# A gated cross-attention and feed-forward block: the down product's way out of PSUM, and its inputs' gather

## The chip, the cores and the metric

The kernel runs on one core of a Trainium2 chip. The metric is the device time of one execution in microseconds (us), lower is better. A core has a tensor engine (PE, with its weight loads PEld), a vector engine (DVE), a scalar engine (ACT), a general engine (POOL) and a sync engine (SP), each with its own queue of instructions, and DMA queues.

## What is computed

The inputs are `x` and a context, each of 8 batches of 256 rows by 512 channels, four 512 x 512 attention weights with biases, and three feed-forward weights of width 1408 with two index lists. Cut to what matters:

```
x = x + tanh(g_xattn) * cross_attention(layernorm(x), context)     # 16 heads, int8-like projections
x = x + tanh(g_ffn)   * ffn(layernorm(x))

ffn(x), rows flattened to 2048 x 512:
    qx, sx, sc = quantise(x, up_index)         # channels reordered, fp8 grid, one scale for each row
    g = (qx*sx) @ (gate weights)^T * sc        # both reordered and quantised, a scale for each column
    u = (qx*sx) @ (up weights)^T * sc
    t = silu(g) * u                            # 2048 x 1408
    qt, st, sct = quantise(t, down_index)      # fp8 grid, st: one scale for each row
    y = (qt*st) @ (qw*w_scale)^T * sct         # w_scale: one scale for each column of y
```

So the last product is multiplied by a number for each row, `st`, and by a number for each column, `w_scale`, and then added to the residual `x`.

## The kernel before

The kernel has two stages. In the first, a loop over batches and pairs of heads computes the attention, and between its steps it prepares the feed-forward weights and, for each batch, the quantised input of the feed-forward part (`quantise_x2`, L743). That input is transposed (channels on partitions), and `store` (L767) writes it to a scratch tensor in device memory, `scr_x[b]`, of 512 channels by 256 rows in bf16.

The second stage is the loop from L1029 over tiles of 128 rows, t = 0 to 15, two tiles to a batch, with two more turns to drain. Three tiles are in work at once. In turn t the kernel does the gate and up products of tile t, the quantisation of tile t-1 and the down product of tile t-2. The order in each engine's queue is the order of the list `steps`: the handles `pe`, `dve`, `act`, `pool` (class `InOrder`) keep the program's order. Instructions outside of these handles, those of the attention's end (`behind_heads`, one step after each turn), are placed between them by the framework. The steps:

- `gather_x` (L912): channels in the order of the index list are fetched from `scr_x[b]` into the tile `xg` by an indirect DMA from POOL's queue; four for a batch, each of 128 channels by 256 rows. Two are issued in each turn, for a tile three turns later; six stand ahead of the loop. `xg` has three buffers.
- `product` (L927): PE, 704 of the 1408 columns at a time, into one of two PSUM buffers of two banks.
- `scaled` (L942): DVE takes a product out of PSUM with the row's scale and the columns' scales (`s_gate`, `s_up`).
- `silu` (L955) on ACT, `sl`; then `gated` (L960) on POOL multiplies it with `s_up` into `tt`.
- `largest` (L971), DVE: `mxt`, the largest magnitude of each row of `tt`; `st`, the scale; `rs_t`, its reciprocal; and `sy`, `st` times the constant UNIT.
- `grid_parts` (L983), ACT: `v_t` and `a_t`. `grid_whole` (L990), DVE: `q_t` and `qt`, the quantised rows.
- `turned` (L997): PE transposes `qt` into PSUM (`ptq`), ACT copies it out as `qtT` in two pieces.
- `down` (L1007): PE, 11 matmuls into one PSUM bank, `yp`.
- `finished` (L1015): DVE takes `yp` out of PSUM, times `sy` of the row, times `scales["down"]` of the column, into `yo`; POOL adds the residual; SP's queue sends 128 rows to the output.

Some order within turn t, as far as the change touches it: first halves of `scaled`, `silu`, `gated`; `gather_x`; `largest` and `grid_parts` of t-1; `down` of t-2; second halves; `grid_whole` and `turned` of t-1; last `finished` of t-2.

`down_scales` (L852) prepares the column scales in the first stage, times the tanh of the gate.

Of the kernel before, what the change touches and what calls it, by code (L numbers as in the profile page):

```python
# [29 lines left out]
F32 = mybir.dt.float32  # L30
BF16 = mybir.dt.bfloat16
# [3 lines left out]
AF = mybir.ActivationFunctionType  # L35
ALU = mybir.AluOpType
# [4 lines left out]
P = 128  # L41
# [4 lines left out]
R448 = 1.0 / 448.0  # L46
F8_MAX = 240.0
UNIT = 1.0 / (F8_MAX / 2) ** 2
# [18 lines left out]
def tile_flamingo_block(  # L67
# [22 lines left out]
    nc = tc.nc  # L90
    B, S, C = x.shape
# [4 lines left out]
    KC = C // P  # L96
    IC = I // P
    TPB = S // P
# [12 lines left out]
    dram = ctx.enter_context(tc.tile_pool(name="dram", bufs=1, space=DRAM))  # L111

    def ctile(shape, name, dt=F32):
        return const.tile(shape, dt, tag=name, name=name)
# [9 lines left out]
    gate = ctile([P, 2], "gate")  # L124
# [26 lines left out]
    for k in range(IC):  # L151
        nc.gpsimd.indirect_dma_start(
            out=dd_i[:, k : k + 1],
            out_offset=None,
            in_=down_idx.rearrange("(r e) -> r e", e=1),
# [14 lines left out]
    }  # L170
    scr_d = dram.tile([I, C], BF16, tag="scr_d", name="scr_d")
    held_d = [dram.tile([I, 1], BF16, tag=f"held{k}", name=f"held{k}") for k in range(IC)]
    scr_x = [dram.tile([C, S], BF16, tag=f"scr_x{b}", name=f"scr_x{b}") for b in range(B)]

    def fp8_grid(rp, src, rs, dst, n, name, v_bufs=3):

        v = rp.tile([P, n], F32, tag="r_v", name=f"v_{name}", bufs=v_bufs)
        nc.scalar.activation(v, src, AF.Identity, scale=rs)
        a = rp.tile([P, n], FP8, tag="r_a", name=f"a_{name}")
        nc.scalar.activation(a, v, AF.Abs, scale=0.5, saturate=False)  # L180
        q = rp.tile([P, n], FP8, tag="r_q", name=f"q_{name}")
        nc.vector.tensor_scalar(q, v, F8_MAX, -F8_MAX, ALU.min, ALU.max, saturate=False)
        nc.vector.scalar_tensor_tensor(dst, a, F8_MAX / 2, q, ALU.max, ALU.mult)

    def scale_of(pool, mx, s, name):

        nc.vector.tensor_scalar(s, mx, R448, None, ALU.mult)
        rs = pool.tile([P, s.shape[-1]], F32, tag="rs", name=f"rs_{name}")
        nc.vector.reciprocal(rs, s)
        return rs  # L190
# [8 lines left out]
    def absmax(dst, src):  # L199
        nc.vector.tensor_reduce(dst, src, AX.X, ALU.max, apply_absolute_value=True)  # L200
# [7 lines left out]
    scales = {}  # L208

    def two_banks(name):  # L210
        return ps_h.tile([P, 2, 512], F32, tag="h", name=name)
# [5 lines left out]
    with ExitStack() as actx:  # L217
# [525 lines left out]
        def quantise_x2(b):  # L743

            xT = tl.tile([P, KC, S], BF16, tag="x2T", name=f"x2T_{b}", bufs=1)

            def rows(nt):
                t = b * TPB + nt
                st = sm.tile([P, 6], F32, tag="st", name=f"st2_{t}")
                nc.vector.bn_stats(st, x_sb[:, t, :])  # L750
                mv = sm.tile([P, 2], F32, tag="mv", name=f"mv2_{t}")
                nc.vector.bn_aggr(mv, st)
                nc.vector.tensor_copy(var2[:, t : t + 1], mv[:, 1:2])
                xm = tl.tile([P, C], F32, tag="xm", name=f"xm_{t}", bufs=1)
                nc.vector.scalar_tensor_tensor(  # L755
                    xm, x_sb[:, t, :], mv[:, 0:1], mu_b, ALU.subtract, ALU.mult
                )
                mx = sm.tile([P, 1], F32, tag="mx", name=f"mx2_{t}")
                absmax(mx, xm)
                rs = scale_of(sm, mx, mx2[:, t : t + 1], f"x2_{t}")  # L760
                q2 = tl.tile([P, C], BF16, tag="q8", name=f"q2_{t}", bufs=4)
                fp8_grid(rp, xm, rs, q2, C, f"x2_{t}")
                return partial(
                    transpose_bf16, q2, xT[:, :, nt * P : (nt + 1) * P], KC, f"x2_{t}"
                )

            def store():  # L767
                nc.sync.dma_start(scr_x[b].rearrange("(k p) n -> p k n", p=P), xT)

            return behind([partial(rows, nt) for nt in range(TPB)]) + [store]  # L770

# [80 lines left out]
        def down_scales():  # L852
            scales["down"] = sd_b = wp.tile([P, C], F32, tag="wqT", name="sd_b")
            row_bcast(sd_b, s_d, "sd")
            nc.vector.tensor_scalar(sd_b, sd_b, gate[:, 1:2], None, ALU.mult)

# [1 line left out]
        for g in range(B * NP + 2):  # L860
            b, i = divmod(g, NP)
# [34 lines left out]


    with ExitStack() as fctx:
        fx = fctx.enter_context(tc.tile_pool(name="fx", bufs=3))
        fw = fctx.enter_context(tc.tile_pool(name="fw", bufs=2))  # L900
        fs = fctx.enter_context(tc.tile_pool(name="fs", bufs=4))
        pe, dve, act, pool = (
            InOrder(tc, e) for e in (nc.tensor, nc.vector, nc.scalar, nc.gpsimd)
        )
        HI = I // 2
        QI = HI // 2
        xg, tiles = {}, [{} for _ in range(NT)]
# [1 line left out]
        def two(a):  # L909
            return a.rearrange("p (j q) -> p j q", q=QI)  # L910

        def gather_x(t):  # L912

            b, nt = divmod(t, TPB)
            if b >= B:
                return
            if nt == 0:
                xg[b] = fx.tile([P, KC, S], BF16, tag="xg", name=f"xg_{b}")
            for k in range(nt * KC // TPB, (nt + 1) * KC // TPB):
                pool.indirect_dma_start(  # L920
                    out=xg[b][:, k, :],
                    out_offset=None,
                    in_=scr_x[b][:, :],
                    in_offset=bass.IndirectOffsetOnAxis(ap=u_i[:, k : k + 1].bitcast(U32), axis=0),
                )

        def product(t, n, half):  # L927
            b, nt = divmod(t, TPB)
            ph = two_banks(f"p_{n}_{t}_{half}")
            for j in range(2):  # L930
                c0 = half * HI + j * QI
                for k in range(KC):
                    pe.matmul(
                        ph[:, j, :QI],
                        xg[b][:, k, nt * P : (nt + 1) * P],
                        wT[n][:, k, c0 : c0 + QI],
                        start=(k == 0),
                        stop=(k == KC - 1),
                    )
            tiles[t][n, half] = ph  # L940
# [30 lines left out]
        def largest(t):  # L971

            h = tiles[t]
            mx = fs.tile([P, 1], F32, tag="mx", name=f"mxt_{t}")
            dve.tensor_reduce(mx, h["tt"], AX.X, ALU.max, apply_absolute_value=True)
            st = fs.tile([P, 1], F32, tag="st", name=f"st_{t}")
            dve.tensor_scalar(st, mx, R448, None, ALU.mult)
            h["rs"] = fs.tile([P, 1], F32, tag="rs", name=f"rs_t_{t}")
            dve.reciprocal(h["rs"], st)
            h["sy"] = fs.tile([P, 1], F32, tag="sy", name=f"sy_{t}")  # L980
            dve.tensor_scalar(h["sy"], st, UNIT, None, ALU.mult)

        def grid_parts(t):  # L983
            h = tiles[t]
# [30 lines left out]
        def finished(t):  # L1015
            h = tiles[t]
            yo = fw.tile([P, C], F32, tag="yo", name=f"yo_{t}")
            dve.scalar_tensor_tensor(
                yo, h["py"], h["sy"], scales["down"], ALU.mult, ALU.mult
            )  # L1020
            pool.tensor_tensor(yo, yo, x_sb[:, t, :], ALU.add)
            nc.sync.dma_start(of[t * P : (t + 1) * P, :], yo)
            tiles[t] = None

        for t in range(TPB + 1):
            gather_x(t)
        product(0, "gate", 0)
        product(0, "up", 0)
        for t in range(NT + 2):  # L1029
            a, b, c = t < NT, 0 <= t - 1 < NT, 0 <= t - 2 < NT  # L1030
            d = a and t + 1 < NT
            steps = [
                (a, scaled, t, "gate", 0),
                (a, product, t, "gate", 1),
                (a, silu, t, 0),
                (a, scaled, t, "up", 0),
                (a, product, t, "up", 1),
                (a, gated, t, 0),
                (a, gather_x, t + TPB + 1),
                (b, largest, t - 1),  # L1040
                (b, grid_parts, t - 1),
                (c, down, t - 2),
                (a, scaled, t, "gate", 1),
                (d, product, t + 1, "gate", 0),
                (a, silu, t, 1),
                (a, scaled, t, "up", 1),
                (d, product, t + 1, "up", 0),
                (a, gated, t, 1),
                (b, grid_whole, t - 1),
                (b, turned, t - 1),  # L1050
                (c, finished, t - 2),
            ]
            for due, f, *args in steps:
                if due:
                    f(*args)
            if t < len(behind_heads):
                behind_heads[t]()
# [51 lines left out]
```

## Time and profile before

| | us |
|---|---|
| median of 3 runs (lowest, highest) | 666.72 (664.53, 668.69) |
| the profiled execution | 663.05 |
| its span on the core | 661.3 |
| windows 573.5 to 627.0 (tiles in undisturbed turns) | 53.50; DVE busy 50.55, PE 48.57, POOL 42.36, ACT 33.64 |
| first instruction of a tile's product in the loop | 476.5 |
| last DMA issued | 652.6 |

In the span from 476 to 653 us, POOL's groups are: `tt` 32 times, 64.8 us busy in all (mean 2025 ns); the gathers, 26 of the 32, 29.0 us (mean 1116); the residual sums `yo` 16 times, 20.2 us (mean 1266). DVE's `yo` are 16 of 743 ns, `sy` 16 of 133 ns.

How to read the profile: its page gives the busy time of each engine, its share of the span and the number of instructions. A line of the timeline is an instruction or a run of like ones: start, duration (both us from the span's start), engine, line, operation, what is written and read (`out<-in`) with partitions x elements and types, and in brackets how long the engine was idle before it and what released it. Instructions issued by a helper carry the helper's line: all steps of the second stage show L61. Durations of neighbours on DVE and ACT overlap a little, so that costs are better read from start to start.

### The profile page before, as it was taken

To read this page: it belongs to the slowest core of one execution; us is meant where nothing else is said; L and a number is where in the kernel's file an instruction comes from. 1 tells how busy PE (TensorE), PEld (TensorE's weight loads), DVE (VectorE), ACT (ScalarE), POOL (GpSimd) and SP (SyncE) were. 2 spreads that over 40 slices of the span, in tenths; PEclk is the share of its full clock that TensorE was granted. 3 is DMA by queue.
4 is the path that set the end of the run, shared out by engine and by line. 5 is a ranking of instruction groups with operands and counts; after the bars stand their busy time and mean duration, and the time that the engine had idled before them with its cause. 6 is when DMAs were issued, how large, how long until landed. Compare 5 with 4: busy or idle time off the path is not lost.

```text
span 661.3 us, 10435 instructions
## 1 busy us (share of the span) xinstructions
PE 519.1 (79%) x3591; PEld 336.7 (51%) x3591; DVE 523.9 (79%) x1405; ACT 428.4 (65%) x995; POOL 273.4 (41%) x236
## 2 busy tenths in 40 slices
PE   2697787978986996996899695896568786899962
PEld 1565555645843753663575464484345453555530
DVE  1996887598658689789749799889589997999970
ACT  1468978729847966984884797575646556556650
POOL 3454263343342331343122001441366875788541
PEclk9798997995995997798699797999698997999986
DMA  8941022002241200301141210320100010111000
GB/s 220 365 87 34 2 79 65 17 16 67 70 152 48 66 16 17 97 17 32 40 168 63 74 55 35 112 81 2 40 17 25 32 48 24 57 49 33 33 32 32
DMA packets 28268, 41.65 MB, mean 63 GB/s; under 512 B 7884, under 2 KB 15436, under 8 KB 28215
## 3 DMA queue, kind: packets, MB, share of 16 engines
q1 hardware_dynamic: 19974, 28.25, 12.9%
q0 software_dynamic: 4656, 12.20, 6.6%
q10 hardware_dynamic: 3584, 0.54, 0.6%
q8 instruction: 28, 0.46, 0.3%
q14 instruction: 26, 0.20, 0.1%
HBM read 30.33 MB, written 10.65 MB: 62 GB/s over the span
## 4 chain that ended last, share of the span: by engine, by line
DVE 34%; PE 30%; ACT 17%; issue 9%; DMA 4%; POOL 3%; SPq 1%; POOLq 0%; ACTq 0%; DVEq 0%
ACT pr L623 6%; PE pk L486 5%; PE t L639 5%; DVE sn L613 3%; DVE mxt L61 3%; PE pv L502 3%; PE s L598 2%; PE poT L657 2%; ACT pT L648 2%; PE p_gate L61 2%; DVE s_gate L61 2%; PE p_up L61 2%; DVE s_up L61 2%; DVE xm L755 2%; ACT v_t L61 2%
## 5 line engine op out<-in xcount | busy, mean ns | idle before, releaser
L623 ACT ACTIVATE pr<-sn,nm 128x256 f32<-128x256 f32 x256 | 127.6, 504 | 44.9 <-DVE nm L613 44.5
L613 DVE CUSTOM_DVE_ANT_0 sn<-s,mk 128x256 f32<-128x256 f32 x256 | 97.9, 417 | 16.2 <-ACT pr L623 10.0
L639 PE MATMUL t<-ident,pr 128*128 128x128 f32 x512 | 79.6, 299 | 19.9 <-DVE v L509 11.8
L598 PE MATMUL s<-kT,qT 32*128 32x256 f32 x512 | 62.3, 484 | 32.3 <-DVE nm L613 22.7
L61 POOL TENSOR_TENSOR tt<-s_up,sl 128x704 f32<-128x704 f32 x32 | 64.8, 2025 | 45.0 <-ACT sl L61 35.2
L639 PEld LDWEIGHTS t<-ident,pr 128*128 128x128 f32 x512 | 62.5, 153 | 34.9 <-DVE v L509 13.4
L61 PEld LDWEIGHTS <-xg 128*128 128x128 bf16 x512 | 50.8, 100 | 53.2 <-issue 13.0
L648 ACT COPY pT<-t 128x512 f32<-128x512 f32 x120 | 65.2, 585 | 13.7 <-PE t L639 13.6
L486 PE MATMUL pk<-cT,wkT 128*128 128x256 f32 x256 | 66.8, 414 | 6.4 <-ACT cT L479 3.5
L61 PE MATMUL p_gate<-gateT,xg 128*128 128x352 bf16 x256 | 45.7, 324 | 21.4 <-DVE s_gate L61 21.4
L486 PEld LDWEIGHTS pk<-cT,wkT 128*128 128x128 f32 x256 | 50.9, 206 | 20.8 <-ACT kT L493 4.1
L738 POOL TENSOR_TENSOR x_sb<-x_sb,bo_b 128x512 f32<-128x512 f32 x16 | 22.8, 1435 | 90.1 <-ACT xq L527 90.1
L598 PEld LDWEIGHTS s<-kT,qT 32*128 32x128 f32 x512 | 34.9, 220 | 48.1 <-issue 31.2
L502 PE MATMUL pv<-wvT,cT 128*128 128x512 f32 x128 | 58.3, 600 | 0.0
L562 POOL TENSOR_SCALAR qT<-qT,bq_c 128x256 f32<-128x256 f32 x32 | 17.9, 565 | 87.4 <-DVE qT L559 65.7
L623 ACT ACTIVATION_READ_ACCUMULATOR pr<-sn,nm 128x1 f32 x256 | 49.6, 194 | 0.0
L61 PE MATMUL yp<-wdT,qtT 128*128 128x512 bf16 x176 | 44.5, 406 | 1.7 <-ACT qtT L61 1.7
L61 PE MATMUL p_up<-upT,xg 128*128 128x352 bf16 x256 | 44.8, 319 | 0.0
L61 ACT COPY qtT<-ptq 128x1024 bf16<-128x1024 bf16 (+1 forms) x32 | 22.3, 749 | 32.3 <-PE ptq L61 32.3
L61 ACT ACTIVATE v_t<-tt,rs_t 128x1408 f32<-128x1408 f32 x16 | 23.5, 1470 | 28.0 <-DVE sy L61 26.2
L61 POOL DMA_INDIRECT xg<-scr_x,u_i x32 | 35.3, 1104 | 11.1 <-issue 5.8
L657 PE MATMUL poT<-pT,v 128*32 128x256 f32 x512 | 38.4, 423 | 0.5 <-ACT pT L648 0.5
(192 smaller groups left out, 1115.5 us busy)
## 6 DMA issues: line engine op xcount, KB each, us to landing
cr<-in_ctx_dram SPq DMA_DIRECT2D x8, 512.0 KB
x_sb<-in_x_dram SPq DMA_DIRECT2D x8, 512.0 KB
out_dram<-yo SPq DMA_DIRECT2D x16, 256.0 KB
wd<-in_L_ffn_w_down_dram SPq DMA_DIRECT2D x4, 704.0 KB
mk<-in_mask_BxSxS_ff_dram SPq DMA_DIRECT2D x8, 256.0 KB
scr_x<-x2T SPq DMA_DIRECT2D x8, 256.0 KB
scr_gate<-gateT SPq DMA_DIRECT2D x1, 1408.0 KB
scr_up<-upT SPq DMA_DIRECT2D x1, 1408.0 KB
```

What stands on the lines that cost most here:

```text
L61: return self.tc.keep_in_program_order(method(*args, **kwargs))
L486: nc.tensor.matmul(pk[:, :L], wTf["k"][:, cc, oc * P : (oc + 1) * P], cT[:, cc, :], start=(cc == 0), stop=(cc == KC - 1),)
L502: nc.tensor.matmul(pv, cT[:, cc, lt * P : (lt + 1) * P], wTf["v"][:, cc, :], start=(cc == 0), stop=(cc == KC - 1),)
L562: nc.gpsimd.tensor_scalar(qT[:, oc, :], qT[:, oc, :], bq_c[:, oc : oc + 1], ISD, ALU.add, ALU.mult)
L598: return nc.tensor.matmul(pss[h][:, nt, :], qT[r0 : r0 + D, oc, nt * P : (nt + 1) * P], kT[r0 : r0 + D, oc, :], start=True, stop=True,)
L613: nc.vector.tensor_tensor_reduce(out=sn[:, nt, :], in0=pss[h][:, nt, :], in1=mk[:, nt, :], scale=-1.0, scalar=3.0e38, op0=ALU.add, op1=ALU ...
L623: nc.scalar.activation(pr[:, nt, :], sn[:, nt, :], AF.Exp, bias=nm[:, nt : nt + 1], scale=-1.0, accum_out=sums[:, nt, h : h + 1],)
L639: nc.tensor.transpose(pst[:, lc, nt * P : (nt + 1) * P], pr[:, nt, lc * P : (lc + 1) * P], ident,)
L648: nc.scalar.copy(pT, pst)
L657: return nc.tensor.matmul(poT[oc][r0 : r0 + D, :], v[0][:, lc, h * D : (h + 1) * D], probsT[h][:, lc, :], start=(lc == 0), stop=(lc == LC ...
L738: nc.gpsimd.tensor_tensor(x_sb[:, t, :], x_sb[:, t, :], bo_b, ALU.add)
L755: nc.vector.scalar_tensor_tensor(xm, x_sb[:, t, :], mv[:, 0:1], mu_b, ALU.subtract, ALU.mult)
```

## The change

The down product leaves PSUM on ACT instead of DVE: an Identity activation with the row's scale `st`. POOL then multiplies by the columns' scales, in place, and adds the residual as before. The constant UNIT goes from the row's scale (`sy` is gone) into the columns' scales, as the second operation of the instruction that applies the gate. The scratch tensors hold two batches side by side (512 channels x 2 x 256 rows), so that one indirect DMA fetches 128 channels of two batches: `xg` has two buffers of twice the size. Of these gathers four stand ahead of the loop, and two each in the turns 1, 2, 5, 6, 9 and 10.

```diff
-    scr_x = [dram.tile([C, S], BF16, tag=f"scr_x{b}", name=f"scr_x{b}") for b in range(B)]
+    scr_x = [
+        dram.tile([C, 2, S], BF16, tag=f"scr_x{b}", name=f"scr_x{b}") for b in range(B // 2)
+    ]
...
-                nc.sync.dma_start(scr_x[b].rearrange("(k p) n -> p k n", p=P), xT)
+                nc.sync.dma_start(
+                    scr_x[b // 2][:, b % 2, :].rearrange("(k p) n -> p k n", p=P), xT
+                )
...
-            nc.vector.tensor_scalar(sd_b, sd_b, gate[:, 1:2], None, ALU.mult)
+            nc.vector.tensor_scalar(sd_b, sd_b, gate[:, 1:2], UNIT, ALU.mult, ALU.mult)
...
-        fx = fctx.enter_context(tc.tile_pool(name="fx", bufs=3))
+        fx = fctx.enter_context(tc.tile_pool(name="fx", bufs=2))
...
-        def gather_x(t):
-
-            b, nt = divmod(t, TPB)
-            if b >= B:
-                return
-            if nt == 0:
-                xg[b] = fx.tile([P, KC, S], BF16, tag="xg", name=f"xg_{b}")
-            for k in range(nt * KC // TPB, (nt + 1) * KC // TPB):
+        def gather_x(j, k0, k1):
+
+            if k0 == 0:
+                xg[j] = fx.tile([P, KC, 2, S], BF16, tag="xg", name=f"xg_{j}")
+            for k in range(k0, k1):
                 pool.indirect_dma_start(
-                    out=xg[b][:, k, :],
+                    out=xg[j][:, k, :, :].rearrange("p b n -> p (b n)"),
                     out_offset=None,
-                    in_=scr_x[b][:, :],
+                    in_=scr_x[j].rearrange("c b n -> c (b n)"),
                     in_offset=bass.IndirectOffsetOnAxis(ap=u_i[:, k : k + 1].bitcast(U32), axis=0),
                 )
...
-                        xg[b][:, k, nt * P : (nt + 1) * P],
+                        xg[b // 2][:, k, b % 2, nt * P : (nt + 1) * P],
...
-            st = fs.tile([P, 1], F32, tag="st", name=f"st_{t}")
-            dve.tensor_scalar(st, mx, R448, None, ALU.mult)
+            h["st"] = fs.tile([P, 1], F32, tag="st", name=f"st_{t}")
+            dve.tensor_scalar(h["st"], mx, R448, None, ALU.mult)
             h["rs"] = fs.tile([P, 1], F32, tag="rs", name=f"rs_t_{t}")
-            dve.reciprocal(h["rs"], st)
-            h["sy"] = fs.tile([P, 1], F32, tag="sy", name=f"sy_{t}")
-            dve.tensor_scalar(h["sy"], st, UNIT, None, ALU.mult)
+            dve.reciprocal(h["rs"], h["st"])
...
             yo = fw.tile([P, C], F32, tag="yo", name=f"yo_{t}")
-            dve.scalar_tensor_tensor(
-                yo, h["py"], h["sy"], scales["down"], ALU.mult, ALU.mult
-            )
+            act.activation(yo, h["py"], AF.Identity, scale=h["st"])
+            pool.tensor_tensor(yo, yo, scales["down"], ALU.mult)
             pool.tensor_tensor(yo, yo, x_sb[:, t, :], ALU.add)
...
-        for t in range(TPB + 1):
-            gather_x(t)
+        gather_x(0, 0, KC)
...
-                (a, gather_x, t + TPB + 1),
+                (0 < t % 4 < 3 and t // 4 + 1 < B // 2, gather_x, t // 4 + 1, t % 4 * 2 - 2, t % 4 * 2),
```

## The prediction

> **What bounds the kernel now.** I read the page first, then the windows of the last stage, then the timeline of one tile. The page says that the two busiest engines are level and that POOL has room on average:
>
> ```profile
> PE 519.1 (79%) x3591; PEld 336.7 (51%) x3591; DVE 523.9 (79%) x1405; ACT 428.4 (65%) x995; POOL 273.4 (41%) x236
> ```
>
> That mean mixes two stages, and the change touches only the second, the feed-forward loop over 16 tiles (t = 0 to 15, from 476 to 653 us). In the stretch 573.5 to 627 us, six undisturbed tiles, the windows give DVE 50.55 of 53.50 us busy, PE 48.57, POOL 42.36, ACT 33.64. One tile (t = 13) by the timeline; I call the start of its first `s_gate`, 609.13, T:
>
> ```profile
> 609.13 0.94 DVE L61 SCALAR_TENSOR_TENSOR s_gate<-p_gate,s_x,sb_gate 128x704 f32<-128x704 f32 x1
> 609.99 0.94 DVE L61 SCALAR_TENSOR_TENSOR s_up<-p_up,s_x,sb_up 128x704 f32<-128x704 f32 x1
> 610.85 1.61 DVE L61 TENSOR_REDUCE mxt<-tt 128x1 f32<-128x1408 f32 x1
> 612.68 0.16 DVE L61 RECIPROCAL rs_t<-st 128x1 f32<-128x1 f32 x1
> 612.76 0.13 DVE L61 TENSOR_SCALAR sy<-st 128x1 f32<-128x1 f32 x1
> 612.93 1.47 ACT L61 ACTIVATE v_t<-tt,rs_t 128x1408 f32<-128x1408 f32 x1 [1.59 <-DVE sy L61]
> 614.43 1.38 ACT L61 ACTIVATE a_t<-v_t 128x1408 fp8e4<-128x1408 f32 x1
> 614.52 0.88 DVE L61 TENSOR_SCALAR q_t<-v_t 128x1408 fp8e4<-128x1408 f32 x1
> 615.84 1.62 DVE L61 SCALAR_TENSOR_TENSOR qt<-a_t,q_t 128x1408 bf16<-128x1408 fp8e4 x1 [0.44 <-ACT a_t L61]
> 616.57 2.44 POOL L61 TENSOR_TENSOR tt<-s_up,sl 128x704 f32<-128x704 f32 x1 [3.47 <-ACT sl L61]
> 617.38 0.74 DVE L61 SCALAR_TENSOR_TENSOR yo<-yp,sy,sd_b 128x512 f32<-128x512 f32 x1
> 618.05 0.94 DVE L61 SCALAR_TENSOR_TENSOR s_gate<-p_gate,s_x,sb_gate 128x704 f32<-128x704 f32 x1
> 618.18 1.39 ACT L61 COPY qtT<-ptq 128x1024 bf16<-128x1024 bf16 x2 [1.69 <-PE ptq L61]
> 618.97 1.27 POOL L61 TENSOR_TENSOR yo<-yo,x_sb 128x512 f32<-128x512 f32 x1
> ```
>
> The period is 618.05 - 609.13 = 8.92 us and DVE is full except for one gap: `qt` starts 0.03 after ACT's `a_t` ends (615.81), 0.44 after DVE could have. So DVE bounds the tile, with the chain rs, v_t, a_t, qt beside it. POOL's second product `tt` takes 2.44 here against 1.68 where nothing disturbs it: it starts while `qt` runs. That is the second thing to see, since the change gives POOL work. The same conflict with POOL first, and with two POOL operations in a row:
>
> ```profile
> 560.55 3.20 DVE L61 SCALAR_TENSOR_TENSOR qt<-a_t,q_t 128x1408 bf16<-128x1408 fp8e4 x1
> 560.57 1.69 POOL L61 TENSOR_TENSOR tt<-s_up,sl 128x704 f32<-128x704 f32 x1
> ```
> ```profile
> 116.78 2.91 POOL L738 TENSOR_TENSOR x_sb<-x_sb,bo_b 128x512 f32<-128x512 f32 x2 [4.91 <-ACT xq L527]
> 117.08 1.49 DVE L294 TENSOR_SCALAR ri_o<-o,rs_o 128x512 f32<-128x512 f32 x1
> 118.49 1.49 DVE L535 TENSOR_SCALAR qx<-xq 128x512 bf16<-128x512 f32 x1
> ```
>
> `qt` took 3.20 instead of 1.62: it stood still for the whole `tt` (1.69). In the second case DVE's small operations (0.41 alone) took 1.49 each, and both POOL operations together 2.91 instead of 2.54: DVE got in after the first POOL operation although the second was queued, then POOL after that. So the two take turns.
>
> **What the Trainium skill says.** "SBUF — State Buffer", section "Who interferes with whom": DVE operations in a two-port mode, or with two SBUF inputs, and GpSimd operations share one port pair as an exclusive lock for the whole instruction. The trace agrees (3.20 against 1.62). It also says that a DVE operation with one SBUF input is free of it; the trace agrees: `s_gate`, `s_up` (one input in PSUM) and `mxt` keep 0.94 and 1.61 beside POOL. So of DVE's work in a tile only `q_t` and `qt` need the port, and the `yo` that leaves DVE (input in PSUM) never did. "Perfetto Trace Analysis", "Optimizing Scalar/DVE Operations", warns that for this reason offloading from DVE to GpSimd might not help. "ScalarE: Activation LUTs", "Step-by-step: what each stage is for": a per-partition scale goes into the same pass of an ACTIVATE; no run here shows it from PSUM with a scale, see below.
>
> **The change part by part, in one tile.**
> Removed from DVE: `sy`, 0.05 from start to start (612.76 to 612.81), worth nothing, since `qt` waits for `a_t`, whose chain does not hold `sy`; and `yo`, 617.38 to 618.05, 0.67. Alone this gives a period of 8.25.
> Added to ACT: `yo`, 128x512 f32 from PSUM. A COPY of that shape takes 0.585 (L648), of 128x256 0.37 (L669); Identity with a pointer operand at 128x256 0.47 (L493). So 0.585 + 0.10 = 0.68; ends 0.58 and 0.73 (v_x, from SBUF). Its cover: ACT idles 1.6 us before `v_t` and 1.7 before `qtT`. It is queued behind the two `qtT` copies, and behind it wait the next `silu` and with that POOL's `tt`; by the clock below `silu` ends 0.26 before `v_t` is due, and if `yo` took more than that, `v_t`, `a_t` and `qt` would move with it one for one.
> Added to POOL: one 128x512 product, the row of its `yo` sum, 1.27. The second waits for the first on the same engine: I take 0.05 between (DVE shows 0.03 to 0.04). The product waits for ACT, and behind it in POOL's queue stand the sum, the next tile's first `tt`, its gathers and its second `tt`, for which `mxt` waits.
> The clock of the new tile, from T: `ptq` starts 0.14 after T (617.52 less the 617.38 at which `qt` lets the next DVE operation go, which is the new T); `qtT` 0.80; ACT is free 1.28 later, 2.08; `yo` on ACT to 2.76; POOL's product 2.84 to 4.11, sum 4.16 to 5.43, first `tt` after that (its silu ends 3.5). Before, that `tt` ran from 2.29 to 3.97, clear of everything. DVE asks for the port for `q_t` at 5.34. It waits for the sum, runs 5.43 to 6.23; `tt` waits, runs 6.23 to 7.90; `qt`, ready at 6.71, waits until 7.90 and lets go at 9.43. The second `tt` (asked 7.87) runs then, until 1.65 after the new T, just ahead of `mxt` at 1.72. So the period is about 9.42, not 8.25: +0.50 against before. The sum behind it: on the port `q_t` 0.8, `qt` 1.53, two `tt` 3.36, two `yo` 2.54 and the time from 1.65 to 2.84 in which POOL waits for qt, ptq, qtT and yo in turn.
> Seven tiles, t = 9 to 15: 7 x 0.50 = +3.5.
> Tiles 2 to 8 carry the rest of the attention and are longer. `yo` on DVE is on the path in t = 5 and 7 (-0.67 each); in 3 and 4 DVE waits for `py` (L727, behind `ptq`) anyway, in 6 for ACT's table load and Sqrt. Losses: t = 3: POOL's `tt` would run from 511.35 to 513.03, `q_t` wants 511.8, so `qt` lets go 1.2 later; t = 6: ACT's `yo` enters the chain qtT, v_x, table load, +0.7; t = 5: q_x (L182) behind POOL, +0.5; t = 8: +0.3. Together about +1.2, with -1 and +5 as ends, as the port's turns fall.
> End: `yp` ends 650.43, then DVE 0.75, POOL 1.26, DMA at 652.63. New: ACT 0.68, POOL 1.27 twice, 0.05: +1.2. Nothing covers it.
> Gathers: 26 in the loop become 12, twice as long in bytes (128 KB), POOL's time for one taken as before (0.98, and 0.30 between). POOL saves 14 x 1.4 us, in tiles 0, 3, 4, 7, 8, 11, 12. Worth 0: POOL waits 35.2 us for silu in these stages. What it costs: in t = 9 and 10 two gathers still stand before the second `tt`, which then ends 2.5 after T and delays `mxt` by 0.9; `q_t` and `qt` come that much later and miss the first `tt`, so the period stays 9.4. Landing 2.6 us before; up to the 4.2 of `gateT`, first used two tiles later. The last pair waits for batch 7's store, issued at 568.0, gathered after 579; were it late, POOL's `tt` and both `yo` would queue behind it. UNIT in `down_scales`, a longer `st`, and the store's address: 0 (no instruction more; far off the path). Two buffers of 4 KB instead of three of 2: the third pair's buffer is free after tile 3, asked for in 5: 0.
> Sum: 3.5 + 1.2 + 1.2 = +5.9 on the profiled execution's 663.05 (span 661.3 and 1.75 around it): 669.0. That execution lies 3.67 under the median of the runs, so against the median: 666.72 + 5.9 = 672.6.
>
> **Rivals.**
> A, POOL takes two turns. If ACT's `yo` is 0.58, the sum ends at 5.33 and the first `tt` may take the port just before `q_t` asks (5.34). Then `tt` to 7.0, `q_t` to 7.8, the second `tt` (asked at 7.44) to 9.5, `qt` to 11.1: a period of 11.05, 1.6 more, in the tiles with no gather around them (8, 12 to 15): +8.1, 680.7. For it: the tie is 0.1 us wide. Against it: L493's 0.10 for the pointer.
> B, the other side: DVE's relief counts in full. It decides if `q_t` and `qt` find the port free, that is if POOL's product, sum and `tt` end before 5.34 (2.5 us of work from 2.84, not 4.3), or if these operations lock each other less than `qt` at 560.55 did. Then 0.67 in t = 5, 7 and 8 to 15 (10 tiles), 1.6 of the stall at 560.55, in whose tile no gather is left, less 1.2 at the end: -7.1, 659.6. For it: DVE is the bound and ACT and POOL have room on average; against it the rows above.
> C, nothing: long tiles give back what the last seven lose: 667.
>
> **How the numbers follow.** Forecast 0.48 (own range 668.5 to 677.5, by tiles 2 to 8 and ACT's price), A 0.17 (677 to 686), B 0.30 (655 to 664), C 0.05. A measurement of this kernel tells about 1% (6.7 us) from no change. Under 660.0: 0.19 of B. Over 673.4: 0.21 of the forecast and all of A, 0.38. Between: 0.43. The range 658 to 681 leaves out the low end of B (0.10) and the high end of A (0.10).
>
> **What would show it.** Steady period 9.4 from `s_gate` to `s_gate`, with `qt` lasting about 2.7 instead of 1.62 and ending with POOL's first `tt` in front of it; `mxt` not waiting. ACT's `yo` 0.68. A `qt` of 1.62 and a period near 8.25 means B; `qt` after both `tt` and a period near 11 means A. Last DMA 1.2 later after the last `yp`. The forecast is wrong if `q_t` and `qt` run beside POOL undelayed.

## The result, and the profile after

The changed kernel takes 672.40 us in the median of 8 runs (669.70 to 678.34), against 666.32 (663.45 to 668.69) for the kernel before on the same chip: 1.2% slower, ratio 1.0119 with a 95% interval of 1.009 to 1.0148. The profiled execution took 670.81 us, with a span of 669.0; that is 7.7 more than the span before. The medians differ by 6.1.

The page's line of busy times. DVE lost 31 instructions, yet it is busy for as long as before (524.7 against 523.9), ACT and POOL for 9 and 11.5 us more:

```profile
PE 523.3 (78%) x3591; PEld 339.3 (51%) x3591; DVE 524.7 (78%) x1374; ACT 437.4 (65%) x1010; POOL 284.9 (43%) x236
```

The same tile as in the prediction, t = 13, in the timeline of the changed kernel. T, the start of its first `s_gate`, is 615.55; here and below, rows that the reading does not need are left out:

```profile
615.55 0.94 DVE L61 SCALAR_TENSOR_TENSOR s_gate<-p_gate,s_x,sb_gate 128x704 f32<-128x704 f32 x1
616.34 1.39 ACT L61 COPY qtT<-ptq 128x1024 bf16<-128x1024 bf16 x2 [2.61 <-PE ptq L61]
617.62 0.70 ACT L61 ACTIVATE yo<-yp,st 128x512 f32<-128x512 f32 x1
618.40 1.28 POOL L61 TENSOR_TENSOR yo<-yo,sd_b 128x512 f32<-128x512 f32 x1 [1.23 <-ACT yo L61]
619.76 1.27 POOL L61 TENSOR_TENSOR yo<-yo,x_sb 128x512 f32<-128x512 f32 x1
620.90 0.89 DVE L61 TENSOR_SCALAR q_t<-v_t 128x1408 fp8e4<-128x1408 f32 x1
620.99 5.36 POOL L61 TENSOR_TENSOR tt<-s_up,sl 128x704 f32<-128x704 f32 x2
622.26 2.55 DVE L61 SCALAR_TENSOR_TENSOR qt<-a_t,q_t 128x1408 bf16<-128x1408 fp8e4 x1 [0.48 <-ACT a_t L61]
624.73 0.94 DVE L61 SCALAR_TENSOR_TENSOR s_gate<-p_gate,s_x,sb_gate 128x704 f32<-128x704 f32 x1
```

The next `s_gate` comes 9.18 after the first, against 8.92 before. ACT's `yo` starts 2.07 after T, POOL's product 2.85, its sum 4.21, the first `tt` 5.44 (that row counts both products of the tile; the second one starts at 623.29, in the row below). `q_t` asks 5.35 after T and is let through; `qt` is ready at 6.71 and takes 2.55 instead of 1.62, because the first `tt` stands in front of it:

```profile
623.29 3.06 POOL L61 TENSOR_TENSOR tt<-s_up,sl 128x704 f32<-128x704 f32 x1
```

So DVE is counted as busy in `qt` for 0.93 us in which it waits for the port. From t = 9 to the drain the mean of `qt` rose from 1625 to 2341 ns. Over the whole loop the 16 `qt` took 33.0 us instead of 27.5 and the 16 `q_t` 17.9 instead of 14.3: this waiting, 9.1 us, fills most of the 14.0 us that `yo` and `sy` had taken on DVE.

Where the 7.7 us of the span are, by the starts of the tiles' first `s_gate` and the last output DMA:

| stretch | before | after | difference |
|---|---|---|---|
| to the start of t = 2 | 496.62 | 497.06 | +0.44 |
| t = 2 to 8 | 76.84 | 80.10 | +3.26 |
| t = 9 to 14 | 53.50 | 56.75 | +3.25 |
| t = 15 and the drain, to the last output DMA | 25.67 | 27.82 | +2.15 |
| after it | 8.67 | 7.27 | -1.40 |

The first and the last row are within what executions of one kernel differ by: a repeat of the changed kernel (below) reached t = 2 at 502.45, and the stretch after the last output DMA is 7.3 to 7.6 in eight of all ten traces and 8.6 or 8.7 in the other two, the kernel before and the first experiment.

And tile by tile (us from one first `s_gate` to the next), with the repeat and four more of the experiments, each from one profiled execution. The tiles t = 12 to 14, with no gather around them, are called steady here, and t = 15 is a fourth of their kind:

| t | before | after | after, repeat | exit only | no product | earlier exit | shorter product |
|---|---|---|---|---|---|---|---|
| 2 | 9.03 | 8.55 | 8.83 | 8.84 | 8.64 | 8.51 | 8.83 |
| 3 | 11.02 | 15.04 | 14.13 | 12.87 | 11.65 | 11.55 | 14.00 |
| 4 | 11.43 | 12.05 | 11.38 | 11.41 | 11.37 | 11.37 | 11.37 |
| 5 | 9.91 | 9.72 | 9.71 | 9.72 | 9.89 | 10.14 | 9.57 |
| 6 | 14.86 | 16.24 | 16.25 | 16.54 | 15.52 | 14.59 | 15.97 |
| 7 | 11.47 | 8.48 | 10.58 | 8.74 | 9.13 | 10.56 | 8.59 |
| 8 | 9.12 | 10.02 | 9.39 | 10.01 | 9.08 | 8.46 | 9.87 |
| 9 | 8.91 | 9.18 | 9.17 | 10.51 | 8.26 | 8.27 | 9.38 |
| 10 | 8.92 | 10.50 | 10.50 | 10.11 | 9.20 | 9.23 | 10.31 |
| 11 | 8.92 | 9.53 | 9.53 | 10.51 | 9.20 | 9.24 | 9.40 |
| 12 | 8.92 | 9.18 | 9.19 | 9.52 | 8.26 | 8.26 | 10.66 |
| 13 | 8.92 | 9.18 | 9.18 | 9.53 | 8.26 | 8.27 | 10.94 |
| 14 | 8.91 | 9.18 | 9.18 | 9.19 | 8.27 | 8.26 | 10.66 |

The traces also record the clock granted to PE, as a share of full speed. In t = 9 to 14 it was 1.00 before and after, so the difference there is not the clock's.

Two places need their own lines. In t = 3 both of POOL's products of the tile went ahead of DVE's operations, `tt` before `q_t` and the second `tt` before `qt` (2.14 and 2.89 instead of 0.88 and 1.62):

```profile
511.89 1.69 POOL L61 TENSOR_TENSOR tt<-s_up,sl 128x704 f32<-128x704 f32 x1
512.20 2.14 DVE L61 TENSOR_SCALAR q_t<-v_t 128x1408 fp8e4<-128x1408 f32 x1
513.93 1.92 POOL L61 TENSOR_TENSOR tt<-s_up,sl 128x704 f32<-128x704 f32 x1 [0.35 <-ACT sl L61]
514.44 2.89 DVE L61 SCALAR_TENSOR_TENSOR qt<-a_t,q_t 128x1408 bf16<-128x1408 fp8e4 x1
```

In t = 9 and 10 the gathers stand between the two products. The first one of t = 9 starts while the delayed `qt` runs and takes 2.18 instead of 0.94, so the second `tt` is late and the `mxt` of t = 10 waits 2.12 for it:

```profile
582.59 2.34 POOL L61 TENSOR_TENSOR tt<-s_up,sl 128x704 f32<-128x704 f32 x1
583.88 2.54 DVE L61 SCALAR_TENSOR_TENSOR qt<-a_t,q_t 128x1408 bf16<-128x1408 fp8e4 x1 [0.48 <-ACT a_t L61]
585.09 2.18 POOL L61 DMA_INDIRECT xg<-scr_x,u_i  x1 [0.16 <-issue]
587.57 0.95 POOL L61 DMA_INDIRECT xg<-scr_x,u_i  x1 [0.30 <-issue]
588.54 1.69 POOL L61 TENSOR_TENSOR tt<-s_up,sl 128x704 f32<-128x704 f32 x1
590.26 1.62 DVE L61 TENSOR_REDUCE mxt<-tt 128x1 f32<-128x1408 f32 x1 [2.12 <-POOL tt L61]
```

And the end: ACT, then two operations on POOL. From the start of the last `yo` to the last output DMA (661.73: the row of the last two DMAs ends at 662.06, and one takes 0.33) it is 3.4 us, where DVE and one operation on POOL took 2.1 (650.52 to 652.63). The first row is of the kernel before:

```profile
650.52 0.75 DVE L61 SCALAR_TENSOR_TENSOR yo<-yp,sy,sd_b 128x512 f32<-128x512 f32 x1 [6.36 <-issue]
```
```profile
658.34 0.69 ACT L61 ACTIVATE yo<-yp,st 128x512 f32<-128x512 f32 x1 [3.87 <-issue]
659.10 1.26 POOL L61 TENSOR_TENSOR yo<-yo,sd_b 128x512 f32<-128x512 f32 x1 [1.95 <-ACT yo L61]
660.44 1.26 POOL L61 TENSOR_TENSOR yo<-yo,x_sb 128x512 f32<-128x512 f32 x1
```

### The profile page after: what moved, and what is told of

Read it like the earlier page. It is cut to its first block, busy times and chain, and to the rows that moved or that the text cites. A ratio compares the mean times of both kernels' runs of the same rounds, so it can differ in the third digit from the quotient of the medians.

```text
span 669.0 us, 10407 instructions
## 1 busy us (share of the span) xinstructions
PE 523.3 (78%) x3591; PEld 339.3 (51%) x3591; DVE 524.7 (78%) x1374; ACT 437.4 (65%) x1010; POOL 284.9 (43%) x236
## 4 chain that ended last, share of the span: by engine, by line
DVE 34%; PE 29%; ACT 18%; issue 7%; POOL 6%; DMA 4%; POOLq 0%; ACTq 0%; SPq 0%; DVEq 0%
ACT pr L625 6%; PE t L641 5%; PE pk L488 5%; DVE sn L615 3%; PE pv L504 3%; PE poT L659 3%; DVE qt L61 3%; ACT pT L650 3%; PE p_gate L61 2%; PE s L600 2%; DVE mxt L61 2%; PE p_up L61 2%; DVE s_gate L61 2%; DVE xm L757 2%; PE py L729 2%
## 5 line engine op out<-in xcount | busy, mean ns | idle before, releaser
L641 PE MATMUL t<-ident,pr 128*128 128x128 f32 x512 | 81.7, 305 | 19.6 <-DVE v L511 11.9
L600 PE MATMUL s<-kT,qT 32*128 32x256 f32 x512 | 63.7, 493 | 31.4 <-DVE nm L615 21.8
L61 POOL TENSOR_TENSOR tt<-s_up,sl 128x704 f32<-128x704 f32 x32 | 70.4, 2205 | 31.9 <-ACT sl L61 19.5
L641 PEld LDWEIGHTS t<-ident,pr 128*128 128x128 f32 x512 | 64.4, 157 | 35.1 <-DVE v L511 13.5
L488 PE MATMUL pk<-cT,wkT 128*128 128x256 f32 x256 | 64.1, 401 | 5.9 <-ACT cT L481 3.5
L61 PE MATMUL p_gate<-gateT,xg 128*128 128x352 bf16 x256 | 48.1, 335 | 16.8 <-DVE s_gate L61 16.2
L488 PEld LDWEIGHTS pk<-cT,wkT 128*128 128x128 f32 x256 | 48.9, 198 | 19.3 <-ACT cT L481 4.1
L564 POOL TENSOR_SCALAR qT<-qT,bq_c 128x256 f32<-128x256 f32 x32 | 17.9, 565 | 87.1 <-DVE qT L561 65.5
L504 PEld LDWEIGHTS pv<-wvT,cT 128*128 128x128 f32 x128 | 23.1, 190 | 26.6 <-issue 24.3
```

What stands on the lines that cost most here:

```text
L61: return self.tc.keep_in_program_order(method(*args, **kwargs))
L488: nc.tensor.matmul(pk[:, :L], wTf["k"][:, cc, oc * P : (oc + 1) * P], cT[:, cc, :], start=(cc == 0), stop=(cc == KC - 1),)
L504: nc.tensor.matmul(pv, cT[:, cc, lt * P : (lt + 1) * P], wTf["v"][:, cc, :], start=(cc == 0), stop=(cc == KC - 1),)
L564: nc.gpsimd.tensor_scalar(qT[:, oc, :], qT[:, oc, :], bq_c[:, oc : oc + 1], ISD, ALU.add, ALU.mult)
L600: return nc.tensor.matmul(pss[h][:, nt, :], qT[r0 : r0 + D, oc, nt * P : (nt + 1) * P], kT[r0 : r0 + D, oc, :], start=True, stop=True,)
L641: nc.tensor.transpose(pst[:, lc, nt * P : (nt + 1) * P], pr[:, nt, lc * P : (lc + 1) * P], ident,)
```

## The experiments

The theory: POOL's added product pushes its first `tt` of a tile into the time in which `q_t` and `qt` need the port that DVE and POOL share; what it costs depends on who asks first. The main rival: POOL and ACT simply have more work, or ACT's exit is what costs, wherever it stands. Each experiment has runs of the kernel before beside it on its chip; the first four ran on one chip (before: median 662.47), the last four on another (666.87), so the ratios are what can be compared. All eight lie within 2% of the kernel before.

**The exit alone.** The kernel before with the change's `finished`, `largest` and `down_scales`, but with its own gathers and buffers:

```diff
-            dve.scalar_tensor_tensor(
-                yo, h["py"], h["sy"], scales["down"], ALU.mult, ALU.mult
-            )
+            act.activation(yo, h["py"], AF.Identity, scale=h["st"])
+            pool.tensor_tensor(yo, yo, scales["down"], ALU.mult)
```

> The new way out of PSUM alone, with the gathers of before (two in each turn to t = 12). Port theory (POOL's column product moves its first tt of a tile from 2.3 to 5.5 us after the tile's start, into the time in which DVE's q_t and qt need the shared port; gathers that stand between tt and tt then make mxt late): worse than the whole change, 675 to 682 us, with tiles of 10 us and more as long as gathers run (t = 9 to 12) and 9.2 after. Rival (the gathers cost nothing, POOL has room): 672, as the whole change, with 9.2 in t = 11 and 12 too.

Measured 670.61 us, ratio 1.0133 (1.0113 to 1.0152). In the sum the rival's case came: nothing worse than the whole change can be told from this. The tiles say why. t = 9, 11 and 12 are 1.33, 0.98 and 0.34 slower than in the whole change, as expected of the gathers (t = 10 is 0.39 faster). But t = 3 is 2.2 faster than in the change's first profile and 1.3 faster than in its repeat: here the gathers stand between POOL's first and second product and keep the second from overtaking `qt`. So the wider gather gives about 2.6 us in t = 9 to 14 (59.37 against 56.75 together), and about half of that is lost again in t = 3.

**The gather alone.** The changed kernel with the kernel before's `finished`, `largest` and `down_scales`:

```diff
-            act.activation(yo, h["py"], AF.Identity, scale=h["st"])
-            pool.tensor_tensor(yo, yo, scales["down"], ALU.mult)
+            dve.scalar_tensor_tensor(
+                yo, h["py"], h["sy"], scales["down"], ALU.mult, ALU.mult
+            )
```

> The two-batch gather alone, with the way out of PSUM of before (DVE's yo with both scales). Port theory: the steady tile stays at 8.92 us and the time at that of before, 664 to 667; the one gain is tile 7, where qt stood still for 1.6 us beside POOL's tt. Rival (the wider gather itself loses time, by landing late or by standing longer on POOL): 669 or more, with mxt or PE waiting in the tiles after t = 1, 2, 5, 6, 9, 10.

Measured 661.45, ratio 0.9994 (0.9974 to 1.0015): no difference that these runs resolve, with every tile from 9 to 14 at 8.91 to 8.93. By itself the wider gather is hidden. Tile 7 took 11.19 against 11.47: POOL's second `tt` (559.24) again went ahead of `qt` (559.49, 2.90), so the 1.6 us that were to be had there didn't come.

**Without POOL's product.** The columns' scales are not applied.

```diff
             act.activation(yo, h["py"], AF.Identity, scale=h["st"])
-            pool.tensor_tensor(yo, yo, scales["down"], ALU.mult)
             pool.tensor_tensor(yo, yo, x_sb[:, t, :], ALU.add)
```

> The whole change without POOL's product with the column scales: this leaves the columns' scales out of the computation. Port theory: POOL's sum then ends at 4.1 and its first tt at 5.8 us after the tile's start, q_t waits 0.4 at most, qt runs at 6.7 undelayed, so a steady tile of 8.25 to 8.35 us and 659 to 663 in all, 10 under the whole change. Rival (ACT's yo between qtT and silu is what costs, not POOL's product): the tile stays above 8.9 and the time at 669 or more.

Measured 658.35, ratio 0.9942 (0.9915 to 0.9969), 1.8% under the whole change by the ratios; steady tiles 8.26. ACT's `yo` stands where it stood (0.70, between `qtT` and silu), and DVE's relief now counts in full: 0.66 a tile. From the timeline of a tile that starts at T = 606.52:

```profile
610.67 1.68 POOL L61 TENSOR_TENSOR tt<-s_up,sl 128x704 f32<-128x704 f32 x1
611.88 1.22 DVE L61 TENSOR_SCALAR q_t<-v_t 128x1408 fp8e4<-128x1408 f32 x1
613.24 1.62 DVE L61 SCALAR_TENSOR_TENSOR qt<-a_t,q_t 128x1408 bf16<-128x1408 fp8e4 x1
```

POOL's first `tt` now goes ahead of `q_t`, which takes 1.22 instead of 0.88, and `qt` still starts on time and runs 1.62. So the cost lies in POOL's product, not in ACT's exit.

**The same work, earlier.** `finished` of tile t-2 stands before `grid_whole` and `turned` of tile t-1. Nothing else differs from the changed kernel:

```diff
+                (c, finished, t - 2),
                 (b, grid_whole, t - 1),
                 (b, turned, t - 1),
-                (c, finished, t - 2),
```

> The same work, but finished of tile t-2 stands before grid_whole and turned of tile t-1, so that ACT's yo runs in front of qtT, and POOL's product and sum follow its second tt at once, 1.7 to 4.3 us after the tile's start, when DVE needs no port. Port theory: first tt 4.3 to 5.9, q_t about 0.6 late, qt on time: a steady tile of 8.25 to 8.4 us without gathers; the gathers in t = 9 and 10 still make mxt late by 1 to 2 us; in all 661 to 666. Rival (the sum of POOL's and ACT's work sets the pace, not its place): 672 and a tile of 9.2.

Measured 660.56, ratio 0.9969 (0.9943 to 0.9995) to the kernel before. The tile, whose first `s_gate` starts at T = 608.25:

```profile
609.83 1.28 POOL L61 TENSOR_TENSOR yo<-yo,sd_b 128x512 f32<-128x512 f32 x1
611.19 1.27 POOL L61 TENSOR_TENSOR yo<-yo,x_sb 128x512 f32<-128x512 f32 x1
612.42 1.69 POOL L61 TENSOR_TENSOR tt<-s_up,sl 128x704 f32<-128x704 f32 x1
613.61 1.25 DVE L61 TENSOR_SCALAR q_t<-v_t 128x1408 fp8e4<-128x1408 f32 x1
614.97 1.62 DVE L61 SCALAR_TENSOR_TENSOR qt<-a_t,q_t 128x1408 bf16<-128x1408 fp8e4 x1
615.70 2.45 POOL L61 TENSOR_TENSOR tt<-s_up,sl 128x704 f32<-128x704 f32 x1 [1.59 <-ACT sl L61]
```

POOL's product and sum run from 1.58 to 4.21 after T, in the gap in which the port was free; the first `tt` follows at 4.17, `q_t` is 0.4 late, `qt` runs on time and undelayed, and the tile takes 8.27. The same instructions cost 0.9 us more per tile in the one place than in the other. The rival, that the amount of work sets the pace, is out.

**The change once more**, unaltered.

> The changed kernel itself, unaltered, on the chip of the others: 1.2% over before, with steady tiles of 9.18 us (t = 12 to 15) and 10.5 where two gathers stand between POOL's products. If turns on the port are decided by chance, tiles 3 and 12 to 15 should differ between executions; if by the order of arrival, steady tiles repeat to 0.02 us.

Measured 674.44, ratio 1.0099 (1.0068 to 1.0129), which agrees with 1.0119. Steady tiles 9.17 to 9.19 again, t = 10 and 11 10.50 and 9.53 again. But t = 7 took 10.58 instead of 8.48, t = 3 14.13 instead of 15.04 and t = 4 11.38 instead of 12.05. In t = 7 `s_up` waited 1.35 us for PE here and 0.35 in the first profile, so that `qt` came 0.33 after POOL's second `tt` instead of 0.67 before it. Where both ask within some tenths of a us, what comes ahead of them decides the turn, and one tile can differ by 2 us between executions. What came ahead here goes with the clock granted to PE. In t = 7 it was 0.50 for the first 5.2 us in the repeat; in the first profile it was 0.50 for the first 3.3 us and then 0.91. At the end of t = 3 it was 0.50 in the first profile (518.00 to 520.65) and 1.00 in the repeat, and PE's `py` took 1.91 and 1.03. From t = 9 to 14 it was 1.00 in both, and the tiles agree to 0.01.

**A shorter product.** POOL's product covers 448 of 512 columns; the scales of the last 64 are left out.

```diff
-            pool.tensor_tensor(yo, yo, scales["down"], ALU.mult)
+            w = C - 64
+            pool.tensor_tensor(yo[:, :w], yo[:, :w], scales["down"][:, :w], ALU.mult)
```

> The whole change with POOL's column product on 448 of 512 columns: the scales of the last 64 columns are left out. 0.16 us less work for POOL in each tile. Theory of turns: POOL's sum then ends at 5.3 us after the tile's start, its first tt takes the port just before q_t asks (5.35), q_t comes after it, the second tt (asked at 7.4) before qt: steady tiles of 10.7 to 10.9 us instead of 9.18, t = 8 and 12 to 15, and 6 to 9 us more in all than the whole change: less work, slower. Rival (the port is shared in proportion, or DVE goes first whenever it asks): 9.0 to 9.2 and no more than the whole change.

Measured 676.17, ratio 1.0142 (1.0106 to 1.0179), beside 1.0099 for the change on the same chip; the intervals overlap, but the tiles don't: 10.66, 10.94 and 10.66 where the change has 9.18. One of them, T = 605.45:

```profile
608.30 1.15 POOL L61 TENSOR_TENSOR yo<-yo,sd_b 128x448 f32<-128x448 f32 x1 [1.23 <-ACT yo L61]
609.53 1.27 POOL L61 TENSOR_TENSOR yo<-yo,x_sb 128x512 f32<-128x512 f32 x1
610.76 1.68 POOL L61 TENSOR_TENSOR tt<-s_up,sl 128x704 f32<-128x704 f32 x1
610.80 2.38 DVE L61 TENSOR_SCALAR q_t<-v_t 128x1408 fp8e4<-128x1408 f32 x1
612.89 1.81 POOL L61 TENSOR_TENSOR tt<-s_up,sl 128x704 f32<-128x704 f32 x1 [0.46 <-ACT sl L61]
613.30 2.89 DVE L61 SCALAR_TENSOR_TENSOR qt<-a_t,q_t 128x1408 bf16<-128x1408 fp8e4 x1
```

The product is 0.13 shorter, `tt` starts 0.04 before `q_t` instead of 0.09 after it, and both `q_t` and `qt` wait for a whole `tt`, 1.5 and 1.3 us. Less work made these tiles 1.5 to 1.8 us slower: it is the order of arrival. All four steady tiles were hit (t = 15 too: from its `s_gate` at 637.71 to the next DVE operation after `qt`, at 648.37, it is 10.66); t = 8 was not (9.87). The four make some 6.2 us; by the ratios the whole is only 0.4% (2.9 us) above the change, less than the 6 to 9 expected: t = 7 took 8.59 here and 10.58 in the repeat of the change, and whole times resolve it badly: their intervals are wide, and the two profiled executions differ by 4.3 us before t = 2 alone (498.16 and 502.45).

**The earlier exit once more**, beside the unaltered change.

> The earlier exit once more beside the unaltered change: 0.3% under before, 1.5% under the change, steady tiles of 8.26 us.

Measured 661.91, ratio 0.9924 (0.9899 to 0.9948); steady tiles 8.26 and 8.27. With 0.9969 from the other chip: 0.3 to 0.8% under the kernel before, and 1.7% under the change here (0.9924 / 1.0099).

**The earlier exit, with the last tile on DVE** and the second pair's gathers ahead of the loop:

```diff
-            act.activation(yo, h["py"], AF.Identity, scale=h["st"])
-            pool.tensor_tensor(yo, yo, scales["down"], ALU.mult)
+            if t < NT - 1:
+                act.activation(yo, h["py"], AF.Identity, scale=h["st"])
+                pool.tensor_tensor(yo, yo, scales["down"], ALU.mult)
+            else:
+                dve.scalar_tensor_tensor(
+                    yo, h["py"], h["st"], scales["down"], ALU.mult, ALU.mult
+                )
...
         gather_x(0, 0, KC)
+        gather_x(1, 0, KC)
```

> The earlier exit, with two things taken back where nothing covers them: the last tile leaves PSUM on DVE with both scales (no product on POOL after the last matmul, 1.3 us), and the gathers of the second pair stand ahead of the loop, where POOL waits anyway. If the last tile's way is on the path, 1.3 us under the earlier exit, 0.5% under before; the gathers in t = 1 and 2 cost nothing before, so moving them gives 0 to 0.5. Rival (the end waits for the output DMA, not for POOL): the same as the earlier exit.

Measured 662.22, ratio 0.9924 (0.9895 to 0.9954): by the time not to be told from the earlier exit. The traces do show the 1.3: from the start of the last `yo` to the end of the last sum it is 2.09 us here, and 3.37 and 3.36 in the two traces of the earlier exit. From the start of t = 15 the last sum ends after 25.39 us, against 26.68 and 25.98; in the second of these PE did the last down product at a granted clock of 0.61 instead of 0.50, and the last `yo` started 0.7 earlier. So the last tile's way through POOL is on the path, but 1.3 us is 0.2%, and the interval of the times is 0.6% wide.

## Why the prediction was right, and where its steps were off

The forecast was 672.6 us, the measurement 672.4, and the likeliest case is what the trace shows: DVE's relief turned into waiting of `qt` for POOL's first `tt`, which the earlier exit and the runs with less or none of POOL's product confirm. That the sum came within 0.2 us is luck. It was made of 3.5 for t = 9 to 15, 1.2 for t = 2 to 8 and 1.2 for the end; between the two profiled executions it is +9.1 to the last output DMA and -1.4 after it, 7.7 in all, while the medians differ by 6.1, and executions of the changed kernel range from 669.7 to 678.3. Errors of opposite sign stand in its terms:

- **`yo` on ACT 0.68, from L493's pointer operand**: 0.70 measured. POOL's product 1.27, started 2.84 after T: 1.28, at 2.85. The time between product and sum, taken as 0.05, was 0.08. This clock decided between forecast and rival A, by the tenth of a us that the forecast said: `tt` came 0.09 after `q_t`.
- **A steady tile of 9.42 (+0.50)**: 9.18 (+0.26). The mis-sized term is how long an operation keeps the port. The forecast let `q_t` wait for the recorded end of the sum (5.43) and `tt` for that of `q_t`. But `q_t`, asked at 5.35 while the sum's record runs to 5.48, took its 0.89 undelayed, and `tt` then lasted from 5.44 to 7.74, 0.6 longer than alone instead of the 0.8 that was taken. Without the product (above), `q_t` was held by 0.34 where the record of `tt` overlapped it by 0.47; with the shorter product `q_t` and `qt` were held by 1.50 and 1.27 for overlaps of 1.64 and 1.40. So the delay is the overlap of the records less some 0.13. For `qt` the sum said 7.90 for its turn; its end, 9.26 less its 1.62, gives 7.64. (Two small readings of the forecast were off: `ri_o` takes 0.47 alone, not 0.41, and at 560.55 the record of `qt` begins 0.02 before that of `tt`, though its 3.20 shows that POOL had the port first.)
- **"so the period stays 9.4" in the tiles with gathers**: wrong. t = 10 took 10.50 and t = 11 9.53. The step took a gather as free of `qt`; a gather that starts while `qt` runs waits for it (2.18). Together t = 9 to 14 came to +3.25 where 6 x 0.50 = 3.0 was forecast: the smaller steady tile and the larger gather tiles cancel.
- **t = 3, +1.2**: +4.0, and +3.1 in the repeat. `tt` went ahead of `q_t` as forecast, but then the forecast let `qt` go next and the trace has POOL's second `tt` next, so `qt` waited for both. The 0.9 between the two executions is `py` at half the granted clock (above), which the forecast could not know.
- **t = 7, -0.67**: -3.0. POOL has no gather left in this tile, and `qt` (565.43, 1.63) went ahead of `tt`. The forecast put this 1.6 us under rival B alone, though it doesn't depend on the port being mild. In the repeat it went the other way (10.58). t = 2, 4, 5, 6 and 8 came to -0.5, +0.6, -0.2, +1.4 and +0.9, for 0, 0, -0.2, +0.7 and +0.3; the +0.6 of t = 4 was gone in the repeat (11.38). Tiles 2 to 8 together: +3.3 for the +1.2 of the sum, inside the ends of -1 and +5.
- **The end, +1.2**: from the start of the last `yp` to the last DMA 7.08 before and 8.18 after, +1.1. The whole stretch from t = 15 to that DMA took 27.82 in the first profile and 26.69 in the repeat, where the clock granted to PE during the last down product was higher (0.76 against 0.54).
- **The gathers at 0**: confirmed alone (0.9994), and not beside POOL's new work: with the exit they are worth 2.6 us in t = 9 to 14.
- **The rivals.** A was the mechanism of t = 3 in the change, and of all steady tiles with the shorter product: 10.66 to 10.94 for the 11.05 forecast. B asked that POOL's three operations end before `q_t`; putting them 1.3 us earlier and taking the wait for `qtT` out of their way gave the 8.26 that B put at 8.25, though the first `tt` still overlaps `q_t` there and costs it 0.4.

## What to carry to other kernels

Before work goes from DVE to POOL, mark in one period the DVE operations that stand still beside POOL (here `q_t` and `qt`), and put POOL's operations beside the others: here the same instructions cost 0.9 us per tile more in one place than in the other, and a 0.13 us shorter one cost 1.5 more, by the order in which both asked. An engine's busy share (POOL's was 41%) says nothing about that; and a stalled DVE operation counts as busy, so compare its duration with its duration alone. What is handed over in a chain (PSUM, ACT, POOL) should be taken when it is ready, not behind the next tile's chain in the same queue: that move alone is the 0.9 us here.

## What the runs showed that was not expected

A gather issued by POOL while DVE's `qt` runs lasts until 0.8 to 0.9 us after the end of `qt`: 2.18 us instead of 0.94 at 585.09, where `qt` ends at 586.42. In the kernel before, one that had started 0.09 before `qt` was not held up (512.47, 0.94), but one that started 0.30 before `q_t` took 1.30 (587.78), while `q_t` kept its 0.88. So having started first does not always save a gather, and which part of it needs what DVE holds stays open.

The delay of an operation that waits for the port is about 0.13 us less than the records overlap: `q_t` kept its 0.89 in the changed kernel although the sum's record overlapped it by 0.13. Whether the holder lets go before its record ends, or the waiting operation needs the port only some time after its record begins, these traces do not tell.

Tiles 2 to 8 and the drain differ between executions of one kernel by as much as the effects in question, with the clock granted to PE: t = 3, 4 and 7 of the changed kernel by 0.9, 0.7 and 2.1 us (in t = 4 the clock was 0.83 and 1.00), the stretch from t = 15 to the last output DMA by 1.1. A single profile of these stretches decides little; t = 9 to 14, with a granted clock of 1.00, repeat to 0.01 us a tile.
